# Two-layer cross attention on one core: values of two groups per second slot, 64-channel rests as 32-column tiles, division on GpSimd, K masks on ScalarE

## The chip, the cores and the metric

The kernel runs on one NeuronCore of a Trainium2 chip. The metric is the device time of one execution in microseconds; lower is better. Three runs of the kernel before took 1022.59, 1025.96 and 1026.53 us, median 1025.96. Names of the engines as the profile gives them: PE is TensorE (matmuls; PEld its weight loads), DVE is VectorE, ACT is ScalarE, POOL is GpSimd, SP is SyncE, which here only issues DMAs.

## What is computed

Two cross-attention layers follow each other on `x` (32 sequences of 256 tokens, 320 channels, 20 heads of 16 channels). Keys and values come from a context of 77 tokens with 512 channels per sequence. All data are fp32.

```python
q = split(x @ Wq); k = split(ctx @ Wk); v = split(ctx @ Wv)      # 20 heads of 16
p = softmax(q @ k.T / sqrt(16))                                  # 256 x 77 per head
x = x + merge(p @ v) @ Wo + bo                                   # once per layer
```

The reference has further branches for context tokens beyond the 77th. There are none in this input, so only this part matters.

## The kernel before, in words

Data are held with channels on the partitions. A *unit* is one layer of one pair of sequences (`NB = 2`), so 16 pairs times 2 layers give 32 units; `units_in_order` starts with four units of layer 0 and then alternates layer 1 of a pair with layer 0 of the pair four ahead. The 320 channels of a pair are two tiles of 128 channels by 512 tokens (both sequences), and a *rest*: 64 channels of the one sequence in partitions 0 to 63 and 64 of the other in 64 to 127. These make five *groups* (`of_group`): four of 128 channels (8 heads, one sequence), and the rest (4 heads of each sequence). The `NG = 5` groups of a unit go through the attention one by one.

The work of a unit is cut into steps:

- `keys` (L219, L228): projects the context, the 256 channels as 128-column tiles and the rest as two 64-column tiles, all into one PSUM bank. The two reads of that bank by DVE (L237) multiply by a mask each (`masks`), so that in `kT[:, e]` only one head of each pair of 16-channel heads is not zero. POOL makes `kM` of it (L240), a copy with -1 in one row of the masked half.
- `queries` (L182, L193) and `queries_rest` (L209): the projection of x, with four banks for the groups 0 to 3 and one for the rest. ACT copies each to `q0`; a DMA then copies `q0` to `q1` (L260).
- `vals` (L273) projects the context by chunks of 128 tokens that run across pairs; ACT copies the result to a stage and DMAs (`place_vals`, L296) bring it to the unit's `v`. The stage holds ones beside the values, so that the product with the probabilities yields the softmax sum as well.
- `maxima` (L309): scores with the tokens on the partitions, in four banks, as four row tiles of 32 channels; DVE reduces each bank to the maximum (L317). When all five groups are done, `turn` transposes the maxima (L326) and eight DMAs (L330) write them into the masked rows of `q0` and `q1`, so that the matmul of `scores` subtracts them.
- `scores` (L343): the transposed scores, again four row tiles and four banks; ACT takes the exponentials (L349) into four `pT` tiles.
- `values` (L363): the product with `v`, four column tiles of 32 columns in one bank `po`. DVE transposes it (L372), inverts the sums (L376), multiplies (L381) and transposes back to `oT` (L387).
- `finish` (L182, L193) and `finish_rest` (L209): the output projection, four banks and one bank; DVE adds bias and residual into x (L394). After layer 1, x goes out by DMA.

A matmul of the rows above works in one of these tile shapes (rows x columns of the array): 128x128 (L193, L219, L273), 64x128 (L182), 128x64 (L209, L228), 32x128 (L309, L343), 128x32 (L363).

The order of the work is written out by hand (`tc.manual_schedule`). `at(slot, where, step)` puts a step into a slot; a unit `u` begins at slot `5u`, and a slot emits its steps in the order load, maxima, turn, scores, values, full, last. With `s = 5u`: keys at s-8, queries at s-7, vals at s-6 (or s-5), the query rest at s-5, maxima at s-6 to s-2, turn at s-2, scores at s to s+4, values one slot after each, finish at s+6 and its rest at s+7. In the steady state each slot has maxima of one unit, scores of the unit before it, values, and then one of: queries; vals; the query rest; finish; keys together with the output rest. Each engine executes its own instructions in the order in which they are emitted, and waits on semaphores for the data and buffers it needs.

All PSUM tiles come from one pool of eight banks (`bank`), which go round in the order of allocation: maxima take four, scores four, values one, keys one, queries and finish four each, a rest or vals one.

Of the kernel before, what the change touches and what calls it, by code (L numbers as in the profile page):

```python
# [51 lines left out]
P = 128  # L54
# [34 lines left out]
def xattn_kernel(ctx: ExitStack, tc: tile.TileContext, xT, cT, cP, weights, outT):  # L89
# [4 lines left out]
    work = ctx.enter_context(tc.tile_pool(name="work", bufs=3))  # L94
    probs = ctx.enter_context(tc.tile_pool(name="probs", bufs=8))
    psum = ctx.enter_context(tc.tile_pool(name="psum", bufs=8, space=bass.MemoryType.PSUM))
# [4 lines left out]
    def bank(name):  # L101
        return psum.tile([P, 512], F32, tag="bank", name=name)
# [3 lines left out]
    def load_x(p):  # L106
        x_sb = io.tile([P, NX], F32, tag="x", name=f"x_{p}", bufs=AHEAD + 4)
        nc.sync.dma_start(out=x_sb, in_=xT[p])
        xs[p] = x_sb
# [90 lines left out]
    def project_rest(ps, w, w22, x):  # L200

        for kc in range(3):
            for b in range(NB):
                r = slice(64 * b, 64 * b + 64)
                if kc < 2:
                    lhsT, rhs = w[:, kc, 2 * P : C], x[:, kc * NT + b * S : kc * NT + (b + 1) * S]
                else:
                    lhsT, rhs = w22[:, 0, r], x[:, 2 * NT : NX]
                nc.tensor.matmul(ps[r, 0:S], lhsT, rhs, start=(kc == 0), stop=(kc == 2))  # L209


    def keys(u):
        p, layer = units[u]
        w, c_sb = w_sb[layer], cs[u]
        kT = st[u]["k"] = work.tile([P, 2, NG, L], F32, tag="kT", name=f"kT_{u}", bufs=3)
        ps = bank(f"psk_{u}")
        for t in range(2):
            for kc in range(NKA):
# [6 lines left out]
                )  # L225
        for kc in range(NKA):
            for b in range(NB):
                nc.tensor.matmul(  # L228
                    ps[64 * b : 64 * b + 64, 4 * L : 5 * L],
                    w["k"][:, kc, 2 * P : C],  # L230
                    c_sb[:, kc, b * L : (b + 1) * L],
                    start=(kc == 0),
                    stop=(kc == NKA - 1),
                )
        src = ps[:, 0 : NG * L].rearrange("p (g k) -> p g k", k=L)
        for e in range(2):
            nc.vector.tensor_scalar_mul(kT[:, e], src, masks[:, e : e + 1])  # L237
        kM = st[u]["km"] = work.tile([P, 2, NG, L], F32, tag="kM", name=f"kM_{u}", bufs=3)
# [111 lines left out]

    def values(u, g):
        vpad = st[u]["v"]
        if g == 0:
            st[u]["o"] = work.tile([P, NX], F32, tag="oT", name=f"oT_{u}", bufs=2)
        po = bank(f"po_{u}_{g}")
        pT = st[u].pop(("p", g))
        for e in range(2):
            for j in range(4):
                if g < 4:
                    b, pair = g % 2, 4 * (g // 2) + j  # L360
                else:
# [6 lines left out]
                    stop=True,  # L368
                )

        turned = work.tile([P, 2 * (S + HD)], F32, tag="turned", name=f"turned_{u}_{g}", bufs=2)
# [8 lines left out]
        normal = work.tile([P, S // 32, 2, HD], F32, tag="normal", name=f"normal_{u}_{g}", bufs=2)  # L380
        nc.vector.tensor_tensor(  # L381
            normal.rearrange("p q e d -> p e q d"),
# [3 lines left out]
        )  # L386
        nc.vector.transpose(of_group(st[u]["o"], g), normal.rearrange("p q e d -> p (q e d)"))  # L387

# [31 lines left out]
    def at(slot, where, step):  # L420
        place.setdefault((slot, where), []).append(step)

    made = [0, 0]
    for u, (p, layer) in enumerate(units):
        s = NG * u
        if layer == 0 and u > 0:
            at(s - 13, "load", lambda p=p: load_x(p))
        if u > 0:
            at(s - 12, "load", lambda u=u: load_context(u))
        at(s - 8, "full", lambda u=u: keys(u))  # L430
        at(s - 7, "last", lambda u=u: queries(u))
        need = range(p * NB * L // P, ((p + 1) * NB * L - 1) // P + 1)
        when = s - 6
        for i in need:
            if i == made[layer]:
                at(s - 9, "load", lambda layer=layer, i=i: load_chunk(layer, i))
                at(when, "last", lambda layer=layer, i=i: vals(layer, i))
                made[layer] += 1
                at(when, "last", lambda u=u, i=i: place_vals(u, i))
                when = s - 5  # L440
            else:
                at(when, "last", lambda u=u, i=i: place_vals(u, i))
        at(s - 5, "full", lambda u=u: queries_rest(u))
        for g in range(NG):
            at(s - 6 + g, "maxima", lambda u=u, g=g: maxima(u, g))
            at(s + g, "scores", lambda u=u, g=g: scores(u, g))
            at(s + g + 1, "values", lambda u=u, g=g: values(u, g))
        at(s - 2, "turn", lambda u=u: turn(u))
        at(s + NG + 1, "last", lambda u=u: finish(u))
        at(s + NG + 2, "last", lambda u=u: finish_rest(u))  # L450


    at(-9, "load", lambda: load_weights(0, "v", "v", nc.scalar))
    at(-4, "load", lambda: load_weights(0, "o", "b", nc.sync))
# [4 lines left out]

    order = ("load", "maxima", "turn", "scores", "values", "full", "last")  # L460
    for slot in range(min(s for s, _ in place), max(s for s, _ in place) + 1):
# [98 lines left out]
```

## Time and profile before

| | |
|---|---|
| median of three runs | 1025.96 us |
| the profiled execution: its own time | 1026.25 us |
| its span, first to last instruction | 1024.5 us |
| granted TensorE clock, mean | 0.993 |
| PE busy | 1011.6 us, 99% of the span |
| PEld busy | 687.8 us, 67% |
| DVE busy | 679.1 us, 66% |
| ACT busy | 404.5 us, 39% |
| POOL busy | 83.4 us, 8% |
| DMA: mean rate | 81 GB/s |

The profile records one execution. A row of its table of groups gives line, engine, operation, output <- inputs, shapes and count; then the time that the group keeps the engine busy and the mean of one; then the engine's idle time ahead of the group and what ended it. fp32 matmuls stand in it as two records each. Matmuls on different tiles of the array run at the same time and are pipelined, so the mean of one is longer than what each adds. The timeline merges neighbouring instructions of one line; its first column is the start, its second the length until the last one ends.

### The profile page before, as it was taken

Reading aid. Unit: us, or ns where it says so; the run is one execution under the profiler, and the core shown is the slowest. Engines: PE = TensorE matmul, PEld = TensorE weight load, DVE = VectorE, ACT = ScalarE, POOL = GpSimd, SP = SyncE. Lnnn points to the kernel's source line nnn. Section 1 sums busy time; section 2 is a strip of 40 time slices with the busy share of each in tenths; the row PEclk is TensorE's granted clock in tenths of the full one; section 3 lists DMA queues with packets and bytes.
Section 4 is the critical chain, followed back from the end, with each engine's and each line's share of the span. In section 5 each row is a group of like instructions: output and inputs, shape, how many; then the busy total and the mean of one; then the engine's idle time right before and its main releaser. Section 6 shows DMA issues by size and latency. Waiting matters only on the chain.

```text
span 1024.5 us, 26952 instructions
## 1 busy us (share of the span) xinstructions
PE 1011.6 (99%) x11328; PEld 687.8 (67%) x11328; DVE 679.1 (66%) x1540; ACT 404.5 (39%) x841; POOL 83.4 (8%) x76
## 2 busy tenths in 40 slices
PE   7999999999999999999999999999999999999988
PEld 6766676666766666766667766666766667666645
DVE  2666666666667666676666676666676666766765
ACT  1344433444333443334443344443334433334442
POOL 2100000000000000000000000000000000000000
PEclk9999999999999999999999999999999999999988
DMA  5622122130222311222121221412223111221111
GB/s 208 232 90 70 47 67 89 54 126 24 87 83 74 120 54 52 94 90 92 55 75 67 85 91 54 134 43 65 87 76 115 50 56 59 84 77 46 62 38 52
DMA packets 53882, 82.51 MB, mean 81 GB/s; under 512 B 15556, under 2 KB 35652, under 8 KB 53762
## 3 DMA queue, kind: packets, MB, share of 16 engines
q1 hardware_dynamic: 53330, 78.96, 23.5%
q8 instruction: 89, 1.46, 0.6%
q10 hardware_dynamic: 432, 1.84, 0.5%
q14 instruction: 31, 0.25, 0.1%
HBM read 35.39 MB, written 10.49 MB: 45 GB/s over the span
## 4 chain that ended last, share of the span: by engine, by line
PE 98%; DMA 1%; DVE 0%; SPq 0%; issue 0%
PE po L363 16%; PE pss L343 14%; PE psy L193 12%; PE psq L193 11%; PE psm L309 11%; PE psv L273 9%; PE psk L219 7%; PE psq L209 5%; PE psy L209 4%; PE psy L182 3%; PE psq L182 3%; PE psk L228 2%; DMA w<-in_w_dram 0%; SPq L330 0%; DMA q<-mT 0%; DVE kT L237 0%
## 5 line engine op out<-in xcount | busy, mean ns | idle before, releaser
L349 ACT ACTIVATE pT<-pss 77x512 f32<-77x512 f32 x640 | 326.9, 590 | 438.3 <-PE pss L343 438.3
L317 DVE TENSOR_REDUCE max<-psm 128x4 f32<-128x308 f32 x640 | 261.2, 470 | 184.2 <-PE psm L309 184.2
L343 PE MATMUL pss<-q,kM 32*77 32x256 f32 x2560 | 174.1, 378 | 3.5 <-DMA q<-mT 3.3
L363 PE MATMUL po<-pT,v 77*32 77x256 f32 x2560 | 174.2, 388 | 0.5 <-DVE max L317 0.5
L240 POOL TENSOR_SCALAR kM<-kT,less 128x385 f32<-128x385 f32 x64 | 79.9, 1260 | 872.5 <-DVE kT L237 872.5
L372 DVE STREAM_TRANSPOSE turned<-po 128x512 f32<-128x512 f32 x160 | 113.4, 709 | 46.6 <-PE po L363 46.3
L309 PEld LDWEIGHTS psm<-kT,q 32*128 32x128 f32 x2560 | 92.0, 183 | 59.6 <-issue 36.5
L309 PE MATMUL psm<-kT,q 32*128 32x154 f32 x2560 | 129.0, 314 | 0.0
L363 PEld LDWEIGHTS po<-pT,v 77*32 77x32 f32 x2560 | 67.7, 109 | 89.9 <-DVE max L317 57.8
L343 PEld LDWEIGHTS pss<-q,kM 32*77 32x77 f32 x2560 | 110.2, 142 | 18.2 <-issue 6.4
L193 PE MATMUL psy<-oT,w 128*128 128x256 f32 x512 | 120.6, 389 | 0.0
L193 PE MATMUL psq<-x,w 128*128 128x256 f32 x512 | 119.1, 386 | 0.0
L193 PEld LDWEIGHTS psy<-oT,w 128*128 128x128 f32 x512 | 95.8, 192 | 23.0 <-issue 11.0
L193 PEld LDWEIGHTS psq<-x,w 128*128 128x128 f32 x512 | 94.6, 190 | 22.2 <-issue 10.6
L394 DVE SCALAR_TENSOR_TENSOR x<-psy,w,x 128x256 f32<-128x256 f32 x160 | 73.8, 483 | 50.6 <-PE psy L193 45.8
L273 PE MATMUL psv<-w,cv 128*128 128x320 f32 (+1 forms) x320 | 96.6, 445 | 0.0
L251 ACT COPY q<-psq 128x256 f32<-128x256 f32 x128 | 47.6, 372 | 97.4 <-PE psq L193 93.6
L219 PE MATMUL psk<-c,w 128*128 128x154 f32 x512 | 77.9, 306 | 5.6 <-DMA w<-in_w_dram 5.6
L219 PEld LDWEIGHTS psk<-c,w 128*128 128x128 f32 x512 | 70.3, 194 | 18.1 <-DVE max L317 12.5
L273 PEld LDWEIGHTS psv<-w,cv 128*128 128x128 f32 (+1 forms) x320 | 56.4, 185 | 35.3 <-DVE max L317 11.9
L387 DVE STREAM_TRANSPOSE oT<-normal 128x256 f32<-128x256 f32 x160 | 71.2, 445 | 5.5
L381 DVE TENSOR_TENSOR normal<-turned,inv 128x256 f32<-128x256 f32 x160 | 67.9, 425 | 5.5
(27 smaller groups left out, 435.8 us busy)
## 6 DMA issues: line engine op xcount, KB each, us to landing
q<-q SPq DMA_DIRECT2D x32, 640.0 KB
x<-in_xT_dram SPq DMA_DIRECT2D x16, 640.0 KB
c<-in_cP_dram SPq DMA_DIRECT2D x32, 308.0 KB
cv<-in_cT_dram SPq DMA_DIRECT2D x38, 256.0 KB
out_dram<-x SPq DMA_DIRECT2D x15, 640.0 KB
v<-stage SPq DMA_DIRECT2D x26, 192.5 KB
q<-mT SPq DMA_DIRECT2D x256, 5.0 KB
w<-in_w_dram ACTq DMA_DIRECT2D x2, 640.0 KB
```

The source lines that it names most:

```text
L193: nc.tensor.matmul(ps[t][b][:, 0:S], w[:, kc, t * P : (t + 1) * P], x[:, i : i + S], start=(kc == 0 and rest_last), stop=(kc == 1 and not ...
L209: nc.tensor.matmul(ps[r, 0:S], lhsT, rhs, start=(kc == 0), stop=(kc == 2))
L219: nc.tensor.matmul(ps[:, t * 2 * L : (t + 1) * 2 * L], w["k"][:, kc, t * P : (t + 1) * P], c_sb[:, kc, :], start=(kc == 0), stop=(kc == NK ...
L240: nc.gpsimd.tensor_scalar_add(kM[:, e], kT[:, e], less[:, e : e + 1])
L273: nc.tensor.matmul(ps[:n, :C], c_sb[:, kc, :n], w_sb[layer]["v"][:, kc, :], start=(kc == 0), stop=(kc == NKA - 1),)
L309: nc.tensor.matmul(ps[j][:, c * 2 * L : (c + 1) * 2 * L], q[r, c * P : (c + 1) * P], kT[r, :, g, :], start=True, stop=True,)
L317: nc.vector.tensor_reduce(mx[:, 2 * g : 2 * g + 2, 2 * j : 2 * j + 2], ps[j][:, : 4 * L].rearrange("p (c e k) -> p c e k", e=2, k=L), AX.X ...
L343: nc.tensor.matmul(ps[j][:L, e * S : (e + 1) * S], kM[r, e, g, :], q[r, :], start=True, stop=True,)
L349: nc.scalar.activation(st[u]["p", g][j][:L], ps[j][:L], AF.Exp, scale=SCALE)
L363: nc.tensor.matmul(po[32 * j : 32 * j + 32, e * S : (e + 1) * S], vpad[:L, b, pair, e].rearrange("p a d -> p (a d)"), pT[j][:L, e * S : (e ...
L372: nc.vector.transpose(turned[:, 0 : 2 * S], po)
L394: nc.vector.scalar_tensor_tensor(x, ps[:, 0:S], w_sb[layer]["b"][:, 0, t : t + 1], x, ALU.add, ALU.add)
```

## The change

Five things are changed together.

- **Values.** `values` is split into `products` (matmuls) and `divide`. Every second slot does the products of two groups, one behind the other, then both divisions; the other slots do none. The pool of probabilities grows from 8 to 12 tiles for it.
- **Rests.** The 64-channel rests of queries, outputs and keys are 32-column tiles, four at a time, in place of two 64-column tiles. They have a place of their own (`rest`) directly behind `values`. The keys' rest is done before the 128-column part of the keys.
- **Division.** The multiplication by the inverse of the sums goes from DVE to POOL; the two transposes to `oT` follow behind both.
- **Masks.** The two masked copies of the keys go from DVE to ACT.
- **Slots.** The steps are dealt over ten slots, two units, with even and odd units in different places: keys at s-7 (even) or s-8 (odd), queries at s-10 or s-7, the query rest at s-5 or s-4, finish at s+6 or s+7, its rest at s+9 or s+10. x is loaded at s-14 in place of s-13, into seven buffers in place of eight.

```diff
@@ -92,7 +93,7 @@
     const = ctx.enter_context(tc.tile_pool(name="const", bufs=1))
     io = ctx.enter_context(tc.tile_pool(name="io", bufs=3))
     work = ctx.enter_context(tc.tile_pool(name="work", bufs=3))
-    probs = ctx.enter_context(tc.tile_pool(name="probs", bufs=8))
+    probs = ctx.enter_context(tc.tile_pool(name="probs", bufs=12))
     psum = ctx.enter_context(tc.tile_pool(name="psum", bufs=8, space=bass.MemoryType.PSUM))
 
     units = units_in_order()
@@ -104,7 +105,7 @@
     xs, cs, cvs = {}, {}, {}
 
     def load_x(p):
-        x_sb = io.tile([P, NX], F32, tag="x", name=f"x_{p}", bufs=AHEAD + 4)
+        x_sb = io.tile([P, NX], F32, tag="x", name=f"x_{p}", bufs=AHEAD + 3)
         nc.sync.dma_start(out=x_sb, in_=xT[p])
         xs[p] = x_sb
 
@@ -200,20 +201,38 @@
     def project_rest(ps, w, w22, x):
 
         for kc in range(3):
-            for b in range(NB):
-                r = slice(64 * b, 64 * b + 64)
+            for i in range(4):
+                b, m = i // 2, i % 2
+                r = slice(32 * i, 32 * i + 32)
                 if kc < 2:
-                    lhsT, rhs = w[:, kc, 2 * P : C], x[:, kc * NT + b * S : kc * NT + (b + 1) * S]
+                    lhsT = w[:, kc, 2 * P + 32 * m : 2 * P + 32 * m + 32]
+                    rhs = x[:, kc * NT + b * S : kc * NT + (b + 1) * S]
                 else:
                     lhsT, rhs = w22[:, 0, r], x[:, 2 * NT : NX]
                 nc.tensor.matmul(ps[r, 0:S], lhsT, rhs, start=(kc == 0), stop=(kc == 2))
 
 
+    def keys_rest(u):
+
+        p, layer = units[u]
+        w, c_sb = w_sb[layer], cs[u]
+        ps = st[u]["psk"] = bank(f"psk_{u}")
+        for kc in range(NKA):
+            for i in range(4):
+                b, m = i // 2, i % 2
+                nc.tensor.matmul(
+                    ps[32 * i : 32 * i + 32, 4 * L : 5 * L],
+                    w["k"][:, kc, 2 * P + 32 * m : 2 * P + 32 * m + 32],
+                    c_sb[:, kc, b * L : (b + 1) * L],
+                    start=(kc == 0),
+                    stop=(kc == NKA - 1),
+                )
+
     def keys(u):
         p, layer = units[u]
         w, c_sb = w_sb[layer], cs[u]
         kT = st[u]["k"] = work.tile([P, 2, NG, L], F32, tag="kT", name=f"kT_{u}", bufs=3)
-        ps = bank(f"psk_{u}")
+        ps = st[u].pop("psk")
         for t in range(2):
             for kc in range(NKA):
                 nc.tensor.matmul(
@@ -223,18 +242,9 @@
                     start=(kc == 0),
                     stop=(kc == NKA - 1),
                 )
-        for kc in range(NKA):
-            for b in range(NB):
-                nc.tensor.matmul(
-                    ps[64 * b : 64 * b + 64, 4 * L : 5 * L],
-                    w["k"][:, kc, 2 * P : C],
-                    c_sb[:, kc, b * L : (b + 1) * L],
-                    start=(kc == 0),
-                    stop=(kc == NKA - 1),
-                )
         src = ps[:, 0 : NG * L].rearrange("p (g k) -> p g k", k=L)
         for e in range(2):
-            nc.vector.tensor_scalar_mul(kT[:, e], src, masks[:, e : e + 1])
+            nc.scalar.activation(kT[:, e], src, AF.Copy, scale=masks[:, e : e + 1])
         kM = st[u]["km"] = work.tile([P, 2, NG, L], F32, tag="kM", name=f"kM_{u}", bufs=3)
         for e in range(2):
             nc.gpsimd.tensor_scalar_add(kM[:, e], kT[:, e], less[:, e : e + 1])
@@ -348,9 +358,9 @@
         for j in range(4):
             nc.scalar.activation(st[u]["p", g][j][:L], ps[j][:L], AF.Exp, scale=SCALE)
 
-    def values(u, g):
+    def products(u, g):
         vpad = st[u]["v"]
-        if g == 0:
+        if "o" not in st[u]:
             st[u]["o"] = work.tile([P, NX], F32, tag="oT", name=f"oT_{u}", bufs=2)
         po = bank(f"po_{u}_{g}")
         pT = st[u].pop(("p", g))
@@ -367,6 +377,9 @@
                     start=True,
                     stop=True,
                 )
+        return po
+
+    def divide(u, g, po):
 
         turned = work.tile([P, 2 * (S + HD)], F32, tag="turned", name=f"turned_{u}_{g}", bufs=2)
         nc.vector.transpose(turned[:, 0 : 2 * S], po)
@@ -378,13 +391,20 @@
         outs = turned.rearrange("p (e n) -> p e n", e=2)[:, :, 0:S]
         outs = outs.rearrange("p e (q r) -> p e q r", r=32)[:, :, :, 0:HD]
         normal = work.tile([P, S // 32, 2, HD], F32, tag="normal", name=f"normal_{u}_{g}", bufs=2)
-        nc.vector.tensor_tensor(
+        nc.gpsimd.tensor_tensor(
             normal.rearrange("p q e d -> p e q d"),
             outs,
             inv.unsqueeze(3).broadcast_to([P, 2, S // 32, HD]),
             ALU.mult,
         )
-        nc.vector.transpose(of_group(st[u]["o"], g), normal.rearrange("p q e d -> p (q e d)"))
+        return normal
+
+    def values(groups):
+
+        po = [products(u, g) for u, g in groups]
+        normal = [divide(u, g, ps) for (u, g), ps in zip(groups, po)]
+        for (u, g), n in zip(groups, normal):
+            nc.vector.transpose(of_group(st[u]["o"], g), n.rearrange("p q e d -> p (q e d)"))
 
 
     def add(u, g, ps):
@@ -423,41 +443,51 @@
     made = [0, 0]
     for u, (p, layer) in enumerate(units):
         s = NG * u
+        odd = u % 2
+        final, ahead = u == NU - 1, u < NU - 2
         if layer == 0 and u > 0:
-            at(s - 13, "load", lambda p=p: load_x(p))
+            at(s - 14, "load", lambda p=p: load_x(p))
         if u > 0:
             at(s - 12, "load", lambda u=u: load_context(u))
-        at(s - 8, "full", lambda u=u: keys(u))
-        at(s - 7, "last", lambda u=u: queries(u))
+        at(s - 8 if odd else s - 7 if u else s - 11, "rest", lambda u=u: keys_rest(u))
+        at(s - 8 if odd else s - 7 if u else s - 11, "full", lambda u=u: keys(u))
+        at(s - 7 if odd else s - 10, "last", lambda u=u: queries(u))
         need = range(p * NB * L // P, ((p + 1) * NB * L - 1) // P + 1)
-        when = s - 6
+        new = [i for i in need if i >= made[layer]]
         for i in need:
-            if i == made[layer]:
-                at(s - 9, "load", lambda layer=layer, i=i: load_chunk(layer, i))
-                at(when, "last", lambda layer=layer, i=i: vals(layer, i))
+            when = s - 6
+            if len(new) == 2 and i == new[1 if odd or u == 0 else 0]:
+                when = s - 4 if odd or u == 0 else s - 9
+            if i in new:
+                at(when - 3, "load", lambda layer=layer, i=i: load_chunk(layer, i))
+                at(when, "full", lambda layer=layer, i=i: vals(layer, i))
                 made[layer] += 1
-                at(when, "last", lambda u=u, i=i: place_vals(u, i))
-                when = s - 5
-            else:
-                at(when, "last", lambda u=u, i=i: place_vals(u, i))
-        at(s - 5, "full", lambda u=u: queries_rest(u))
+            at(when, "full", lambda u=u, i=i: place_vals(u, i))
+        at(s - 4 if odd else s - 5, "rest", lambda u=u: queries_rest(u))
         for g in range(NG):
             at(s - 6 + g, "maxima", lambda u=u, g=g: maxima(u, g))
             at(s + g, "scores", lambda u=u, g=g: scores(u, g))
-            at(s + g + 1, "values", lambda u=u, g=g: values(u, g))
         at(s - 2, "turn", lambda u=u: turn(u))
-        at(s + NG + 1, "last", lambda u=u: finish(u))
-        at(s + NG + 2, "last", lambda u=u: finish_rest(u))
-
-
-    at(-9, "load", lambda: load_weights(0, "v", "v", nc.scalar))
+        if ahead:
+            at(s + 7 if odd else s + 6, "last", lambda u=u: finish(u))
+            at(s + 10 if odd else s + 9, "rest", lambda u=u: finish_rest(u))
+        else:
+            at(NG * NU if final else NG * NU - 1, "last", lambda u=u: finish(u))
+            at(NG * NU if final else NG * NU - 1, "last", lambda u=u: finish_rest(u))
+    groups = [(u, g) for u in range(NU) for g in range(NG)]
+    for n in range(0, len(groups), 2):
+        at(n + 1, "values", lambda n=n: values(groups[max(n - 1, 0) : n + 1]))
+    at(len(groups), "values", lambda: values(groups[-1:]))
+
+
+    at(-10, "load", lambda: load_weights(0, "v", "v", nc.scalar))
     at(-4, "load", lambda: load_weights(0, "o", "b", nc.sync))
     at(1, "load", lambda: load_weights(1, "k", "k", nc.sync))
     at(2, "load", lambda: load_weights(1, "q", "q22", nc.sync))
     at(3, "load", lambda: load_weights(1, "v", "v", nc.sync))
     at(4, "load", lambda: load_weights(1, "o", "b", nc.sync))
 
-    order = ("load", "maxima", "turn", "scores", "values", "full", "last")
+    order = ("load", "maxima", "turn", "scores", "values", "rest", "full", "last")
     for slot in range(min(s for s, _ in place), max(s for s, _ in place) + 1):
         for where in order:
             for step in place.get((slot, where), ()):
```

## The prediction

> **What bounds the kernel now.** I read the page first: the busy shares (section 1) and the chain that ended last (section 4).
>
> ```profile
> PE 1011.6 (99%) x11328; PEld 687.8 (67%) x11328; DVE 679.1 (66%) x1540; ACT 404.5 (39%) x841; POOL 83.4 (8%) x76
> ...
> PE 98%; DMA 1%; DVE 0%; SPq 0%; issue 0%
> ```
>
> PE is busy for 1011.6 of 1024.5 us and is 98% of the chain. The time is therefore the length of PE's stream plus its waits. Next comes the timeline of one steady slot (start, length, engine, line).
>
> ```profile
> 500.34 0.81 PE L309 MATMUL psm<-kT,q 32*128 32x154 f32 x16
> ...
> 500.97 1.04 PE L343 MATMUL pss<-q,kM 32*77 32x256 f32 x16
> 501.16 1.63 DVE L317 TENSOR_REDUCE max<-psm 128x4 f32<-128x308 f32 x4 [1.10 <-PE psm L309]
> ...
> 501.94 1.07 PE L363 MATMUL po<-pT,v 77*32 77x256 f32 x16
> 502.08 2.04 ACT L349 ACTIVATE pT<-pss 77x512 f32<-77x512 f32 x4 [1.21 <-PE pss L343]
> ...
> 502.94 1.52 PE L209 MATMUL psq<-x,w 128*64 128x256 f32 x12
> 503.07 0.72 DVE L372 STREAM_TRANSPOSE turned<-po 128x512 f32<-128x512 f32 x1 [0.28 <-PE po L363]
> ```
>
> From start to start: psm 0.63, pss 0.97, po 1.00 us. The four reads of psm by DVE begin 0.82 after psm and end 2.45 after it (502.79). Before, po (one bank) and what follows it run in that time. The first slots of the kernel show what happens when the cover is missing:
>
> ```profile
> 27.33 0.81 PE L309 MATMUL psm<-kT,q 32*128 32x154 f32 x16
> 27.45 1.15 DVE L237 TENSOR_SCALAR kT<-psk,masks 128x385 f32<-128x385 f32 x2 [0.47 <-PE psk L228]
> ...
> 43.77 0.45 DVE L387 STREAM_TRANSPOSE oT<-normal 128x256 f32<-128x256 f32 x1
> 44.14 1.59 DVE L317 TENSOR_REDUCE max<-psm 128x4 f32<-128x308 f32 x4
> ...
> 44.63 1.07 PE L363 MATMUL po<-pT,v 77*32 77x256 f32 x16 [0.51 <-DVE max L317]
> ```
>
> DVE comes to the maxima late (behind the transpose at 43.77), and PE holds po back 0.51 us until the first read, 44.14 + 0.47, has freed a bank. Banks go round in turn: each of the eight is used again by the eighth allocation after it, so po takes the first bank of psm and a four-bank product directly behind pss takes all four.
>
> **Price of a mode switch.** In the trace's single starts, equal modes run at a round of 216 ns for 256 columns (131 for 154, 66 for 77). A block in a new mode adds one exposed weight load, 104 ns for 128 columns, 51 for 64, 24 for 32, and about 93 to 113 ns to leave: po is 4 x 216 + 24 + 113 = 1001 ns. "TensorEngine Tiling (Array Packing)" of the Trainium skill, Key Properties, says that changing the tiling mode drains TensorE; "TensorE: Matmul & The Clock Gate", LDWEIGHTS, prices a load by its columns over 1.2 GHz (107, 53, 27 ns). The trace agrees with both.
>
> **What the change saves on PE, per two units (ten slots).** Before: 36 switches; after: 27. Values: 10 x 1.001 = 10.01 us become 5 x (8 x 0.216 + 0.024) = 8.76, with nothing to leave, since a 32-column rest in the same mode always follows: -1.25. Rests: 2 x (1.446 + 1.395 + 0.586) = 6.85 become key rests 2 x (8 x 0.066 + 0.11) = 1.28, output rests 2 x 1.296 + 0.113 = 2.71, query rests 2 x 1.409 = 2.82, together 6.81: -0.05. (Four tiles per 66 ns is denser than any row, where two share a round; pairs of load and matmul start 7 ns apart in po, so 4 x 7 fits. If they were held to psm's 131 per four, that is +0.5 us a unit, +17 in all.) Sum -1.30, or -20.8 us for 16 pairs. Projections and vals keep their rows: 1.064 + 3.651 and 2.351.
>
> **What it adds: waits on PE.** Number the ten slots of two units from the one with an even unit's keys; all begin with psm and pss: (1) two values, keys; (2) vals; (3) two values, output and query rests; (4) output product; (5) two values, keys; (6) query product; (7) two values, output rest, vals; (8) query product; (9) two values, query rest; (10) output product.
>
> Slot 2: an even unit's keys now stand directly ahead of its first maxima; before, a slot lay between. The masks go to ACT. Its rows fix the price: 372 ns for 256 elements, 590 for 512 (below), so 480 for 385, the second 0.42 behind the first. At 27.45 the masks begin 0.12 after psm begins; so psm, which needs both, is held 0.12 + 0.42 + 0.48 = 1.0 us. ACT is idle then, so nothing queues ahead.
>
> Slots 4 and 8: four banks directly behind pss. The fourth tile would start 0.63 + 0.97 + 0.54 (two rounds and a load) = 2.14 after psm; its bank is read at 2.45 + 0.03. That is 0.34, and its own weight load (0.107) follows in the open: 0.47 each.
>
> Slot 6: the fourth pss takes the keys' bank of slot 5, which ACT still reads: masks begin 0.12 after where psm begins and end at 1.02; this pss is due at 0.65, and its weights load after: 0.47. Its later maxima reads are then hidden.
>
> Slot 10: slot 9 is short, 0.63 + 0.98 + 1.75 + 1.41 = 4.77 us. Within it DVE turns the first group at 2.74 (1.13 after po, as at 503.07), inverts, turns and inverts the second (0.72 and 0.28 each), done at 4.72. POOL divides by about 5.6, and only then, at 6.05, has DVE moved the result to oT. The next maxima are queued behind that transpose and were due at 4.77 + 0.82 = 5.59. The bank waits grow from 0.47 to about 0.76, and a pss loses 0.12 to the query rest's copy on ACT: 0.88.
>
> Sum: 1.0 + 3 x 0.47 + 0.88 = 3.3 us of waits against 1.3 saved: +2.0 per two units, or about +1.55 in the six pairs with an extra vals block, which lengthens slot 9.
>
> ```profile
> L349 ACT ACTIVATE pT<-pss 77x512 f32<-77x512 f32 x640 | 326.9, 590 | 438.3 <-PE pss L343 438.3
> ...
> L240 POOL TENSOR_SCALAR kM<-kT,less 128x385 f32<-128x385 f32 x64 | 79.9, 1260 | 872.5 <-DVE kT L237 872.5
> ...
> L251 ACT COPY q<-psq 128x256 f32<-128x256 f32 x128 | 47.6, 372 | 97.4 <-PE psq L193 93.6
> ...
> L381 DVE TENSOR_TENSOR normal<-turned,inv 128x256 f32<-128x256 f32 x160 | 67.9, 425 | 5.5
> ```
>
> **The division on POOL** has no row. From below: "GPSIMD Engine Reference", section 3.1, gives 2.6 cycles an element for a two-input op, an estimate of 0.56 us for 256. From above: POOL's own row, 1260/385 = 3.3 ns an element, makes 0.84, and twice that for a second input 1.7. I take 0.85. At 0.6 the total is 2 us better; up to about 1.05 each 0.1 us costs 1 us in all; above it the transposes push the maxima reads in every slot after two values, and 0.1 costs some 5 us: 1.5 is +22. The 68 us taken off DVE and the 37 us of masks are worth nothing by themselves, since DVE is idle a third of the span; ACT's 31 us more are hidden outside slots 2 and 6.
>
> **The rest at nothing.** Loads are issued a slot or three earlier or later on SP; x has seven buffers and is loaded a slot earlier. The tightest is an odd unit's turn: mT is ready 2.95 into slot 9 of its row (here slot 1), eight issues at 0.59 and a landing of 1.3 take 6.0, and pss needs them some 9 us after. SP has nothing longer ahead of it than an issue; if that cover went, 0.6 us per issue ahead of it would be lost once per pair, 9 us. The larger probs pool removes a wait only. The end keeps its stall for the last turn, 3.3 us before and about 4 after.
>
> **Sum.** Ten pairs at +2.0 and five at +1.55 (the first pair fills, the last drains, and these two balance) are +27.7. The profiled 1024.5 us span (1026.25 as timed) becomes 1052; the median of 1025.96 becomes 1054.
>
> **Rivals.** (1) POOL is the bound of the values: a division of 1.2 to 1.7 us holds the two transposes, and behind them the maxima's four reads and the banks. Speaks for it: POOL's 1260 ns row, against the 425 of DVE. Against: only two divisions in two slots. 1060 to 1085. (2) Not slower: PE's bank waits don't come, because a product gets a bank that is free and not the oldest. Then slots 4, 6, 8 and 10 wait for nothing (2.3 us), slot 2's 1.0 stays against 1.30 saved, -0.3 a pair: 1021. It decides once waits are below 1.3 us per pair. Against it stands 44.63, where po waited for the oldest bank. (3) The waits are real but smaller, half of those counted behind pss, since loads and reads overlap more than I assume: +0.9 a pair, 1040. (4) All waits hide: 1005; the step from masks to psm speaks against it.
>
> **How the numbers follow.** My forecast, 1046 to 1060, has 0.58; rival 1 0.18; rival 3, 1031 to 1046, 0.14; rival 2 0.06; rival 4 0.04. About 0.5% (5 us) is what a measurement of this kernel can tell from no change. Faster 0.07, same 0.03, slower 0.90. The range leaves out rivals 2 and 4, the worst of rival 1 and the best of 3: 1037 to 1076.
>
> **What would show it.** In the profile after: po x32 blocks of 1.75 us before the rest with no drain; psm after an even unit's keys waiting about 1 us for kT on ACT; psy and psq waiting for DVE's maxima; a POOL row for normal near 0.85 us; PE's idle and waits near 50 us. Wrong if the psm-to-kT wait is missing, if the products behind pss start without waiting, or if POOL's row is far from 0.85.

## The result and the profile after

The changed kernel takes 1053.79 us (median of four runs, 1053.32 to 1054.29) against 1026.24 us before (median of four, 1022.59 to 1026.59). The ratio of the means is 1.0277, with a 95% interval of 1.0253 to 1.0301: slower, and 0.2 us from the predicted 1054. The profiled span is 1052.1 us against 1024.5. Of twelve further runs of the kernel before, four took 1022.5 to 1022.8 us at a mean granted clock of 0.996 and eight 1025.4 to 1027.5 us at 0.993; its profiled run, at 0.993, is of the second kind (see the last section).

First the page of the changed kernel: the busy shares, the chain that ended last, and from the table of groups the division that has moved to POOL (busy us, mean ns; idle before it and what ended it).

```profile
PE 1020.5 (97%) x12608; PEld 712.4 (68%) x12608; DVE 557.0 (53%) x1316; ACT 438.9 (42%) x905; POOL 183.0 (17%) x236
...
PE 96%; ACT 3%; DMA 1%; issue 0%; SPq 0%; DVE 0%; ACTq 0%
...
L394 POOL TENSOR_TENSOR normal<-turned,inv 128x256 f32<-128x256 f32 x160 | 99.4, 622 | 787.7 <-DVE inv L389 786.6
```

DVE has 122 us less to do than before and POOL 100 more; PE still carries the chain. New in the chain is ACT with 3%. PE's share of the span fell from 99% to 97%, so PE now idles for 31.6 us where it idled for 12.9. The group of the masks and the list of waits say where ACT comes in:

```profile
L247 ACT ACTIVATE kT<-psk,masks 128x385 f32<-128x385 f32 x64 | 33.8, 579 | 91.9 <-PE psk L238 91.9
```

```profile
PE psm L319 <- ACT kT L247: 18.0, 15, 1.2
```

Before, the list had no wait of PE's psm for the masks. Now there are 15, one per pair, 1.2 us each. The other losses do not show as waits of PE, and have to be read from the lengths of blocks: from the start of one block to the start of the next. Two places of the kernel before serve for comparison, an output product (L182, then L193) and the keys (L219, then their rest, L228). The product's first block takes 1.06 us start to start, the keys 2.30:

```profile
505.98 1.07 PE L363 MATMUL po<-pT,v 77*32 77x256 f32 x16
506.98 1.13 PE L182 MATMUL psy<-oT,w 64*128 64x256 f32 x8
508.05 3.72 PE L193 MATMUL psy<-oT,w 128*128 128x256 f32 x16
...
514.36 2.37 PE L219 MATMUL psk<-c,w 128*128 128x154 f32 x16
516.66 0.76 PE L228 MATMUL psk<-c,w 128*64 128x77 f32 x16
```

This is the timeline of the changed kernel, with the slots numbered as in the prediction: slot 2 begins at 508.65, slot 4 at 518.66, slot 5 at 525.45, slot 6 at 531.81, slot 10 at 557.48.

```profile
505.08 2.37 PE L238 MATMUL psk<-c,w 128*128 128x154 f32 x16
...
507.55 1.05 ACT L247 ACTIVATE kT<-psk,masks 128x385 f32<-128x385 f32 x2 [2.74 <-PE psk L238]
...
508.65 0.81 PE L319 MATMUL psm<-kT,q 32*128 32x154 f32 x16 [1.21 <-ACT kT L247]
...
518.66 0.81 PE L319 MATMUL psm<-kT,q 32*128 32x154 f32 x16
...
519.49 1.64 DVE L327 TENSOR_REDUCE max<-psm 128x4 f32<-128x308 f32 x4 [0.67 <-PE psm L319]
...
520.26 1.61 PE L183 MATMUL psy<-oT,w 64*128 64x256 f32 x8
...
521.80 3.72 PE L194 MATMUL psy<-oT,w 128*128 128x256 f32 x16
...
527.11 1.93 PE L373 MATMUL po<-pT,v 77*32 77x256 f32 x32
...
528.86 0.72 PE L223 MATMUL psk<-c,w 128*32 128x77 f32 x32
...
531.98 1.05 ACT L247 ACTIVATE kT<-psk,masks 128x385 f32<-128x385 f32 x2 [2.73 <-PE psk L238]
...
532.44 1.73 PE L353 MATMUL pss<-q,kM 32*77 32x256 f32 x16
...
557.47 0.62 POOL L394 TENSOR_TENSOR normal<-turned,inv 128x256 f32<-128x256 f32 x1 [0.23 <-DVE inv L389]
557.48 0.81 PE L319 MATMUL psm<-kT,q 32*128 32x154 f32 x16
...
558.12 0.45 DVE L407 STREAM_TRANSPOSE oT<-normal 128x256 f32<-128x256 f32 x1 [0.41 <-POOL normal L394]
558.49 1.59 DVE L327 TENSOR_REDUCE max<-psm 128x4 f32<-128x308 f32 x4
...
559.08 1.75 PE L183 MATMUL psy<-oT,w 64*128 64x256 f32 x8
```

- **Slot 2.** The keys end, the masks begin at 507.55 and last 1.05, and psm starts at 508.65, when both are done.
- **Slot 4.** The output product starts behind pss at 520.26, while the reads of the maxima run until 521.13. From its start to the next block at 521.80 it takes 1.54 us, where it took 1.064 before.
- **Slots 5 and 6.** po of two groups takes 1.75 us (527.11 to 528.86), twice 0.864 us of matmuls and 0.024 for one weight load, with nothing lost on leaving the mode, since a rest in the same mode follows. In slot 6 the pss block lasts 1.73 in place of 1.04, because ACT reads the keys' bank until 533.03.
- **Slot 10.** POOL's second division ends at 558.09, DVE's transpose after it begins at 558.12, and the maxima, due 0.82 after psm, start behind that transpose at 558.49, 1.01 after psm. The output product takes 1.69 us (559.08 to 560.77).

Start to start, the blocks that differ over ten slots, in us (each other block is equal within 0.02):

| block | before | after | difference |
|---|---|---|---|
| values of ten groups | 10 x 1.001 | 5 x 1.751 | -1.255 |
| all rests | 6.854 | 6.826 | -0.03 |
| slot 2: last keys block to psm | 2.297 | 3.575 | +1.28 |
| slot 4: L183 | 1.064 | 1.539 | +0.475 |
| slot 6: pss | 0.970 | 1.659 | +0.69 |
| slot 8: L183 | 1.064 | 1.541 | +0.477 |
| slot 10: L183 | 1.064 | 1.692 | +0.63 |
| pss of the other nine slots, some with waits of 0.06 | 8.98 | 8.84 | -0.14 |
| sum | | | +2.13 |

The steady pair of units, psm to psm, is 63.40 us against 61.28, +2.12; a pair with an extra vals block 65.60 against 63.63, +1.97. The fourteen pairs from unit 2 to unit 30 take 901.6 us against 872.1, +29.5. What comes before takes 0.5 more, and what comes after 2.4 less: +27.6 in all.

### The profile page after: what moved, and what is told of

It reads as the page before. It is cut to its first block, busy times and chain, and to the rows that moved or that the text cites. A ratio compares the mean times of both kernels' runs of the same rounds, so it can differ in the third digit from the quotient of the medians.

```text
span 1052.1 us, 29665 instructions
## 1 busy us (share of the span) xinstructions
PE 1020.5 (97%) x12608; PEld 712.4 (68%) x12608; DVE 557.0 (53%) x1316; ACT 438.9 (42%) x905; POOL 183.0 (17%) x236
## 3 DMA queue, kind: packets, MB, share of 16 engines
q8 instruction: 99, 1.62, 0.6%
## 4 chain that ended last, share of the span: by engine, by line
PE 96%; ACT 3%; DMA 1%; issue 0%; SPq 0%; DVE 0%; ACTq 0%
PE po L373 14%; PE pss L353 14%; PE psy L194 11%; PE psq L194 11%; PE psm L319 11%; PE psv L283 9%; PE psk L238 7%; PE psy L183 5%; PE psy L212 4%; PE psq L212 4%; PE psq L183 4%; ACT kT L247 3%; PE psk L223 2%; DMA w<-in_w_dram 0%; SPq L340 0%
## 5 line engine op out<-in xcount | busy, mean ns | idle before, releaser
L394 POOL TENSOR_TENSOR normal<-turned,inv 128x256 f32<-128x256 f32 x160 | 99.4, 622 | 787.7 <-DVE inv L389 786.6
L353 PE MATMUL pss<-q,kM 32*77 32x256 f32 x2560 | 180.3, 377 | 4.5 <-DMA q<-mT 3.8
L373 PE MATMUL po<-pT,v 77*32 77x256 f32 x2560 | 157.5, 385 | 0.0
L319 PE MATMUL psm<-kT,q 32*128 32x154 f32 x2560 | 131.2, 314 | 18.0 <-ACT kT L247 18.0
L353 PEld LDWEIGHTS pss<-q,kM 32*77 32x77 f32 x2560 | 107.1, 141 | 28.8 <-ACT kT L247 7.3
L385 DVE STREAM_TRANSPOSE turned<-po 128x512 f32<-128x512 f32 x160 | 109.5, 685 | 30.5 <-PE po L373 30.5
L373 PEld LDWEIGHTS po<-pT,v 77*32 77x32 f32 x2560 | 75.7, 110 | 72.9 <-DVE max L327 28.8
L250 POOL TENSOR_SCALAR kM<-kT,less 128x385 f32<-128x385 f32 x64 | 80.0, 1263 | 73.1 <-ACT kT L247 73.1
```

What stands on the lines that cost most here:

```text
L319: nc.tensor.matmul(ps[j][:, c * 2 * L : (c + 1) * 2 * L], q[r, c * P : (c + 1) * P], kT[r, :, g, :], start=True, stop=True,)
L353: nc.tensor.matmul(ps[j][:L, e * S : (e + 1) * S], kM[r, e, g, :], q[r, :], start=True, stop=True,)
L373: nc.tensor.matmul(po[32 * j : 32 * j + 32, e * S : (e + 1) * S], vpad[:L, b, pair, e].rearrange("p a d -> p (a d)"), pT[j][:L, e * S : (e ...
L385: nc.vector.transpose(turned[:, 0 : 2 * S], po)
L394: nc.gpsimd.tensor_tensor(normal.rearrange("p q e d -> p e q d"), outs, inv.unsqueeze(3).broadcast_to([P, 2, S // 32, HD]), ALU.mult,)
```

## The experiments

My theory: PE's stream does get shorter, by 1.3 us a pair, but the removed and moved blocks had covered other engines' reads (had kept PE busy while these ran), and PE now waits for the reads: the masks in slots 2 and 6, the maxima's banks in slots 4, 8 and 10. The rivals: POOL's division is what costs; the masks' new engine is what costs; the 32-column rests are slower than taken. Line numbers are those of the changed kernel unless another is named. Ratios are of the means, to the kernel before as it ran beside each (medians 1025.74 to 1026.21 us), with 95% intervals; pair is the steady pair, 61.28 us before and 63.40 after the change.

| run | time, us | ratio | pair, us |
|---|---|---|---|
| values of one group in every slot | 1041.37 | 1.0143 [1.0128, 1.0158] | 62.51 |
| masks on DVE | 1058.46 | 1.0310 [1.0295, 1.0326] | 63.64 |
| division on DVE | 1058.15 | 1.0308 [1.0292, 1.0323] | 63.80 |
| shorter maxima | 1031.33 | 1.0044 [1.0027, 1.0060] | 61.82 |
| before, some rests as 32-column tiles | 1019.42 | 0.9949 [0.9931, 0.9967] | 61.00 |
| before, all rests as 32-column tiles | 1039.18 | 1.0145 [1.0118, 1.0171] | 62.26 |
| division done twice | 1068.38 | 1.0424 [1.0401, 1.0447] | 64.73 |
| even units' keys earlier | 1058.51 | 1.0336 [1.0310, 1.0362] | 63.47 |
| an output rest behind the keys | 1039.32 | 1.0131 [1.0104, 1.0157] | 62.50 |
| the same, shorter maxima | 1014.68 | 0.9891 [0.9870, 0.9912] | 60.78 |
| values of one group, division on DVE | 1041.09 | 1.0149 [1.0130, 1.0168] | 62.51 |

### Values of one group in every slot

```diff
-    for n in range(0, len(groups), 2):
-        at(n + 1, "values", lambda n=n: values(groups[max(n - 1, 0) : n + 1]))
-    at(len(groups), "values", lambda: values(groups[-1:]))
+    for n in range(len(groups)):
+        at(n + 1, "values", lambda n=n: values(groups[n : n + 1]))
```

> Values of one group in every slot again, all else as in the changed kernel. Waits theory (PE waits for PSUM banks behind scores, and for the key masks): a values block stands again between scores and the four-bank products, so the waits of slots 4, 8 and 10 (0.475 + 0.477 + 0.63 us per two units) go, five values blocks pay 0.137 us each for entering and leaving their mode (+0.69), the waits of slots 2 and 6 stay: -0.9 us per two units, about 1040 us. Rival, GpSimd's division bounds the values: the number of divisions is the same, so 1051 to 1057 us.

The time falls by 12.4 us against the changed kernel, 0.89 per pair. The timeline of this run at slot 4:

```profile
512.54 0.81 PE L319 MATMUL psm<-kT,q 32*128 32x154 f32 x16
...
513.36 1.64 DVE L327 TENSOR_REDUCE max<-psm 128x4 f32<-128x308 f32 x4 [0.67 <-PE psm L319]
...
514.14 1.07 PE L373 MATMUL po<-pT,v 77*32 77x256 f32 x16
...
515.14 1.13 PE L183 MATMUL psy<-oT,w 64*128 64x256 f32 x8
...
516.20 3.72 PE L194 MATMUL psy<-oT,w 128*128 128x256 f32 x16
```

The maxima's reads end at 515.00, and po has filled the time until then: L183 is back at 1.06 us. So it is in slots 8 and 10. The blocks give the account of the 0.89: the values cost 5 x 0.888 + 5 x 1.001 = 9.45 in place of 8.76 (+0.69; 0.888 where a rest in the same mode follows), and the three bank waits are gone (0.475 + 0.477 + 0.63 = 1.58). The values of two groups alone are thus a loss of 0.89 a pair, though they save PE 0.69 us of mode switches. Slots 2 and 6 keep their waits of 1.28 and 0.69, as they should.

### Shorter maxima

Each maximum is taken over the first 39 of 77 keys, so that DVE reads half as much; the softmax then subtracts a value that need not be the maximum, and all else stays.

```diff
-                ps[j][:, : 4 * L].rearrange("p (c e k) -> p c e k", e=2, k=L),
+                ps[j][:, : 4 * L].rearrange("p (c e k) -> p c e k", e=2, k=L)[:, :, :, 0:39],
```

> The maxima are reduced over 39 of the 77 keys, so each read of a maxima bank is shorter; the output then subtracts another value than the reference does. Waits theory: a read falls from 0.47 to about 0.31 us and the fourth bank is free some 1.85 us after the maxima begin, before the fourth tile of the products is due at 2.14: the waits of slots 4 and 8 go (0.475 and 0.477 us), most of slot 10's 0.63, the waits for the masks stay: -1.5 us per two units, 1028 to 1033 us. Rival, the division or the mode switches are the loss: 1051 to 1055 us, since neither changes.

22.5 us come back. The timeline of this run at slot 4:

```profile
508.24 0.81 PE L319 MATMUL psm<-kT,q 32*128 32x154 f32 x16
...
509.06 1.00 DVE L327 TENSOR_REDUCE max<-psm 128x4 f32<-128x156 f32 x4 [0.67 <-PE psm L319]
...
509.83 0.73 PEld L183 LDWEIGHTS psy<-oT,w 64*128 64x128 f32 x8 [0.37 <-DVE max L327]
509.83 1.13 PE L183 MATMUL psy<-oT,w 64*128 64x256 f32 x8
...
510.90 3.72 PE L194 MATMUL psy<-oT,w 128*128 128x256 f32 x16
```

No matmul has been taken away or moved, yet L183 takes 1.06 in slots 4, 8 and 10, and the pair is 1.58 shorter, which is the sum of the three bank waits. Slots 2 and 6 are as in the changed kernel (3.57 and 1.66). Note the weight load: its 0.37 "<-DVE max" stands there although nothing is lost now. That label names who released the idle time, not a loss; the length of the block tells.

### Masks on DVE, division on DVE

```diff
-            nc.scalar.activation(kT[:, e], src, AF.Copy, scale=masks[:, e : e + 1])
+            nc.vector.tensor_scalar_mul(kT[:, e], src, masks[:, e : e + 1])
```

> Key masks back on VectorE, all else as in the changed kernel. Waits theory: the 1.28 us in slot 2 come from the place of the keys, directly ahead of the maxima that read them; VectorE's two masks last 1.15 us against ScalarE's 1.05, so the wait stays or grows by 0.1 to 0.3 us, and VectorE's reads of the maxima come later: 1054 to 1061 us. Rival, the move of the masks to ScalarE is the loss: 16 waits of 1.28 us go, 1033 us.

```diff
-        nc.gpsimd.tensor_tensor(
+        nc.vector.tensor_tensor(
```

> Division back on VectorE, all else as in the changed kernel. Waits theory: the chain of two groups on VectorE grows from some 3.2 to 3.8 us, so the maxima reads behind it come later and slot 10 waits about 0.4 us more: 1056 to 1063 us. Rival, GpSimd's division is the loss (622 ns against 425, and two hand-overs): faster than the changed kernel, 1030 to 1047 us.

Each of the two moves of engine is worth something in this kernel: 0.24 a pair for the masks, 0.40 for the division. With the masks on DVE, keys to psm in slot 2 takes 3.70 and pss in slot 6 takes 1.75. The wait is the same as in the changed kernel and only has another engine's name in the waits of this run:

```profile
PE psm L319 <- DVE kT L247: 19.9, 15, 1.3
```

So neither new engine causes the loss: each move gives back a little of it. With the division on DVE the two transposes of slot 9 end later still, the maxima of slot 10 begin 1.42 us after psm instead of 1.01, and slot 10 alone holds the 0.40.

### The division done twice

POOL does every division two times.

```diff
+        nc.gpsimd.tensor_tensor(
+            normal.rearrange("p q e d -> p e q d"),
+            outs,
+            inv.unsqueeze(3).broadcast_to([P, 2, S // 32, HD]),
+            ALU.mult,
+        )
```

> The changed kernel with each division done twice on GpSimd, so that it lasts 1.24 us in place of 0.62. Waits theory: the transposes behind it come 0.9 to 1.2 us later, hidden in most slots, in the open in slot 10 and where the next slot begins soon: 1062 to 1075 us. Rival, GpSimd bounds the values: two divisions every second slot add 1.24 us to each such slot, five in ten slots: about 1150 us.

14.6 us more for 0.62 us more per division. DVE now waits for POOL (the waits of this run; DVE's are in total, times, longest), behind it the maxima come late, and slot 4 and slot 10 show it: pss 1.66 and 1.92 us in place of 0.97. In slot 4 the product behind it gives 0.39 back (1.15 in place of 1.54), so slot 10 has most of the 1.33 a pair.

```profile
DVE oT L413 <- POOL normal L400: 112.4, 158, 1.4
```

At 1.24 us per division, POOL is the cost that rival 1 meant. At the 0.622 that it really takes, it is not.

### Values of one group, division on DVE

The first edit and the division's edit together.

> Values of one group in every slot, and the division back on VectorE. Waits theory: with values between scores and products nothing waits for the end of that chain, so the division's engine makes no difference: 1038 to 1044 us, as with one group per slot and GpSimd. Rival, the hand-over to GpSimd costs time of its own: 1030 us or less.

62.51 us per pair with either engine. Where the values stand between scores and products, one division per slot is hidden on DVE as on POOL. The 0.40 above goes with two groups per slot; whether it is the second division or the missing block between scores and products that brings it out, these runs do not separate.

### The rests alone, in the kernel before

Both runs start from the kernel before. All rests become 32-column tiles as in the change; those of keys and queries go to a place `rest` directly behind values. In the first run the output rest stays in `last`, behind the keys; in the second it too goes to `rest`, ahead of the keys.

```diff
+        at(s - 8, "rest", lambda u=u: keys_rest(u))
         at(s - 8, "full", lambda u=u: keys(u))
...
-        at(s - 5, "full", lambda u=u: queries_rest(u))
+        at(s - 5, "rest", lambda u=u: queries_rest(u))
...
-        at(s + NG + 2, "last", lambda u=u: finish_rest(u))
+        at(s + NG + 2, "rest" if u < NU - 2 else "last", lambda u=u: finish_rest(u))
```

The last pair of lines is in the second run only; the new tiles themselves are left out of this cut.

> The kernel before, with one part alone: the rests of keys, queries and outputs as 32-column tiles, those of keys and queries directly behind values, the output rest still behind the keys; values, masks and division as before. Waits theory: the query rest saves values' exit and a weight load (0.16 us a unit), the keys' rest about as much as the output rest then pays to enter a mode of its own (0.02 left), and the banks are read as early as before: -0.17 us a unit, 1020 to 1021.5 us. Rival, four 32-column tiles cost TensorE more than two of 64: 1027 us or more.

> As the run before it, but the output rest too stands directly behind values, ahead of the keys, so that the keys end the slot. Waits theory: TensorE's work shrinks by 0.34 us a unit (11 us), but the fourth scores bank of the next slot is the keys' bank, which VectorE reads only then: a wait of 0.6 to 0.7 us in each of 32 units (20 us): 1034 to 1039 us. Rival, mode switches alone decide: 1015 us.

The difference between the two is one place in the order: 19.8 us. The timeline of the second run, in the slot after the keys (L236 keys, L245 masks, still on DVE, L317 psm, L351 pss):

```profile
524.12 0.81 PE L317 MATMUL psm<-kT,q 32*128 32x154 f32 x16
524.30 1.14 DVE L245 TENSOR_SCALAR kT<-psk,masks 128x385 f32<-128x385 f32 x2 [1.87 <-PE psk L236]
524.75 0.60 PE L351 MATMUL pss<-q,kM 32*77 32x256 f32 x6
...
525.59 1.05 PE L351 MATMUL pss<-q,kM 32*77 32x256 f32 x10 [0.24 <-DVE kT L245]
...
526.57 1.07 PE L371 MATMUL po<-pT,v 77*32 77x256 f32 x16
```

With the output rest behind them, the keys' masks ran while PE worked on that rest. With the keys last, the masks run into the next slot, pss needs the keys' bank, and the block grows from 1.06 us in the first run to 1.82 (524.75 to 526.57) in each unit. Both times fall just outside what was expected: the first 0.6 us below the range, the second 0.2 above it, its wait being 0.77 a unit and not 0.6 to 0.7. The 32-column form is not the cost: with the cover left in place it gains 0.28 a pair. That run, 1019.42 us with a ratio of 0.9949 [0.9931, 0.9967], is faster than both kernels, by half a per cent than the one before. About 4.1 us of its span's gain lie in the fourteen pairs and 3.0 in the tail, where the clock matters (last section).

### The keys moved, or covered

The first run moves the even units' keys two slots earlier, from slot 1 to slot 9, so that two slots stand between them and their maxima, where one did before the change. The second puts the odd units' output rest behind the keys of slot 1, where it covers the masks.

```diff
-        at(s - 8 if odd else s - 7 if u else s - 11, "rest", lambda u=u: keys_rest(u))
-        at(s - 8 if odd else s - 7 if u else s - 11, "full", lambda u=u: keys(u))
+        at(s - 8 if odd else s - 9 if u else s - 11, "rest", lambda u=u: keys_rest(u))
+        at(s - 8 if odd else s - 9 if u else s - 11, "full", lambda u=u: keys(u))
```

> The changed kernel with the keys of even units two slots earlier, in slot 9, so that no maxima follow them at once. Waits theory: slot 2's 1.28 us go, but the cover is moved and not made: slot 1 then holds nothing behind its two values, so that the next slot's maxima wait for VectorE's transposes, and slot 10's scores wait for the keys' bank as slot 6's do: 1048 to 1062 us. Rival, the wait for the masks can be taken away for itself: 1033 us.

```diff
-            at(s + 10 if odd else s + 9, "rest", lambda u=u: finish_rest(u))
+            at(s + 8 if odd else s + 9, "last" if odd else "rest", lambda u=u: finish_rest(u))
```

> The changed kernel with one step moved: the output rest of odd units goes from slot 3 to the end of slot 1, behind the keys of the even unit, so that 1.3 us of matmuls lie between those keys and the maxima that read their masks. Waits theory: the 1.28 us of slot 2 go; the rest now enters and leaves its mode for itself (+0.14), and slot 3 is as short as slot 9, so slot 4 waits as slot 10 does (0.475 to 0.63): -1.0 us per two units, 1037 to 1041 us. Rival, the cover is only moved once more, as with the keys in slot 9: 1050 us or more.

Moving gives nothing. Keys to psm is back at 2.30 us, but two other waits take its place. In slot 10, now directly behind the keys, pss takes 1.65 in place of 0.97 us, as it does in slot 6: it waits for the keys' bank. The product of slot 10 is then back at 1.06. In slot 2 the wait is of another kind. Slot 1 holds nothing behind its two values any more, so DVE comes to the maxima of slot 2 only behind the transposes of both groups, and the vals block, which takes the first bank of these maxima, starts 2.26 us after pss in place of 0.97:

```profile
510.26 1.44 PE L353 MATMUL pss<-q,kM 32*77 32x256 f32 x16
...
511.08 1.02 DVE L407 STREAM_TRANSPOSE oT<-normal 128x256 f32<-128x256 f32 x2 [0.23 <-POOL normal L394]
...
512.02 1.60 DVE L327 TENSOR_REDUCE max<-psm 128x4 f32<-128x308 f32 x4
...
512.52 2.42 PE L283 MATMUL psv<-w,cv 128*128 128x320 f32 x8 [0.82 <-DVE max L327]
```

So the keys in slot 1 had themselves covered the turning of two groups. In every order tried here, the masks' 1 us on the bank is hidden only by PE work behind the keys that takes no bank of theirs. Covering works: keys to the next block is 2.30 again, and of the 15 waits of psm one is left in the waits of this run:

```profile
PE psm L319 <- ACT kT L247: 1.1, 1, 1.1
```

1.28 are gained, and 0.13 + 0.15 + 0.09 given back (the rest pays for its own mode, 1.43 in place of 1.30; slot 4's L183 takes 1.69 in place of 1.54, since slot 3 is now as short as slot 9; pss in slot 2 takes 1.06 in place of 0.97): 0.90 a pair.

### An output rest behind the keys, and shorter maxima

The edit just above together with the maxima over 39 of 77 keys.

> The same move, and the maxima reduced over 39 of 77 keys (the output then subtracts another value than the reference does), so that both kinds of waits go at once and only slot 6's 0.69 us stays. Waits theory: what TensorE saves by the change (1.28 us per two units, less 0.14 here) stands out: 1.58 + 1.28 - 0.14 = -2.7 us per two units against the changed kernel, 1009 to 1017 us, faster than the kernel before. Rival, the saving of mode switches isn't there: 1020 us or more.

With four of the five waits away, all but slot 6's 0.69, the kernel takes 1014.68 us, 0.9891 [0.9870, 0.9912] of the time before. The pair is 60.78, 0.50 below the kernel before: -1.28 for the array, +0.13 for the rest's mode, +0.69 and +0.09 for pss in slots 6 and 2, -0.14 for the short waits in pss, which is -0.51. So the array's saving is there in full, and the waits alone had turned it over. Of its gain in the span, 5.1 us are the fourteen pairs and 7.0 the tail, about 3.4 of which are worth the clock's shorter stretch at half (last section). No run took slot 6's wait away; that it is the keys' bank rests on the timeline, on the run that put keys ahead of slot 10, and on the two runs with the rests alone.

## Why the prediction was right

- **The bound.** PE's stream plus its waits: held. PE is 96% of the chain after, and the runs that took waits away moved the pair by what those waits measured.
- **The array's saving.** Predicted -1.30, measured -1.28. Double values 1.751 each (8.76 predicted for five, 8.755 measured); key rests 0.650 (0.638 predicted, so four tiles do share 66 ns, and the doubt of +17 us was not needed); output rests 1.297 and 1.410, query rests 1.41.
- **Slots 4 and 8.** Predicted 0.47 each, measured 0.475 and 0.477. (The prediction's two terms, 0.34 and 0.107, add to 0.45.) The trace of before shows neither; the rule of banks in turn, read from one stall of 0.51 us at the kernel's start, gave them.
- **Slots 2 and 6: mechanism right, size too low.** Predicted 1.0 and 0.47, measured 1.28 and 0.69. The mis-sized term is the masks: I took 0.42 + 0.48 = 0.90 us from ACT's copies, and it is 1.05 (579 ns each); they also begin 0.17, not 0.12, after psm could have started (507.55, against 505.08 + 2.30).
- **Slot 10: size too high.** Predicted 0.88, measured 0.63. One mis-sized term is POOL's division, taken at 0.85 and measured at 0.622, which touches the prediction's own sign of being wrong, a row far from 0.85. Another is the pss ahead of the product, which was to lose 0.12 to a copy on ACT: it takes 0.969 us and loses nothing. And the step from the late maxima to 0.76 does not follow from the terms: maxima 0.46 late on top of a wait of 0.45 make 0.91. With the 0.19 that they were late (1.01 against 0.82) the same sum gives 0.64, and it measured 0.63; with the division on DVE they were 0.60 late, the sum gives 1.05, and the two blocks together lost 1.03. So the mechanism held, and the 0.88 was nearer than its own terms make it. The estimate of 0.56 us from "GPSIMD Engine Reference", section 3.1, of the Trainium skill was nearer than my reading of POOL's own row; that row is of a different operation.
- **Pairs with an extra vals block.** Predicted +1.55, measured +1.97. Slot 10 had only 0.63 to give back there, not 0.88, and gave 0.15.
- **The sum of the waits.** Predicted 3.3, measured 3.55.
- **The ends.** The forecast's +27.7 for fifteen pairs is, in proportion, +25.9 for the fourteen that were measured, at +29.5; so the pairs came 3.6 us dearer. What lies around them, the fifteenth pair among it, was forecast at +1.8 and measured at -1.9 (+0.5 at the start, -2.4 in the tail), 3.7 cheaper. That the total agrees within 0.2 us is luck: these two errors cancel, and the clock is part of the second.
- **"Worth nothing by themselves".** Said of the work taken off DVE. Wrong in the small: the division on POOL is worth 0.40 and the masks on ACT 0.24 a pair here, because DVE is needed at once for the maxima just when two groups are turned. In the order with one group per slot, the division's engine is worth nothing.
- **The price of a slow POOL.** The prediction's two slopes (1 us for each 0.1 up to 1.05, 5 us beyond) make +14 from 0.622 to 1.24; the doubled division cost 14.6.
- **The rivals.** A POOL bound fell with the doubled division; no bank waits, half of them, and all waits hidden fell with the shorter maxima, which gave back 1.58 a pair, the whole of the three.

What I would read differently: the masks on ACT should have been bounded from both sides, as the division was. A copy with a scale per partition had no row, and I priced it as a plain one.

## What to carry to other kernels

Removing a mode switch or a block on the engine that bounds a kernel is worth its time only if no one had used that time: before doing so, list per slot which banks the next block takes in turn, and when their readers end. A short block between a producer and the next multi-bank user is cover, and its place matters more than its form: in the kernel before, 32-column rests gain 0.28 us a pair with the output rest behind the keys and lose 0.98 with it ahead of them. Where several edits come together, price them apart: here the rests' form alone was a gain in the kernel before, and two groups per slot and keys at the end of a slot were the loss.

## What the runs showed of the hardware

- **ACT's masked copy.** 128x385 from PSUM with a scale per partition takes 579 ns, where a line through ACT's copies (372 ns for 256) and exponentials (590 for 512) gives 480. DVE needs 615 for the same (the run with the masks on DVE). Where the extra 99 ns come from was not tried.
- **POOL's two kinds.** The two-input product of 256 elements takes 622 ns, 2.4 ns an element; the one-input operation with a scalar per partition 1263 ns for 385, 3.3 an element. Of these two, the one with more inputs was not the dearer per element.
- **The clock in the tail.** In the kernel before, PE idles at the last turn of the maxima in two gaps of 1.67 and 1.62 us, and from the start of the second, at 989.5, the trace shows the clock at half for 13.7 us. In the changed kernel, with gaps of 2.11 and 1.73 us, the stretch is 6.8 us, as in the run with some rests as 32-column tiles; in the run with an output rest behind the keys it is 3.4, and the longest gap there is 1.73; with shorter maxima besides, it is 6.8, and the longest gap 1.53. All are multiples of about 3.4 us. The gaps of 1.2 us, one per pair, that the changed kernel has for the masks left the clock at full. The 6.8 us less at half clock are worth 3.4 us of PE's work, more than the whole difference in the tail (-2.4). Why the stretch was shorter was not tried.
